# Two rotations of four PSUM banks in place of one of eight, in a context attention of small heads

## The chip, the cores and the metric

The kernel runs on one core of a Trainium2 chip. The metric is device time in microseconds (us) from one launch to its end, and the number compared is the median of several runs. The engines are TensorE (PE in the profile; its weight loads are shown apart as PEld), VectorE (DVE), ScalarE (ACT), GpSimd (POOL) and SyncE (SP), which issues the DMAs. Each engine takes its own instructions in order and waits on semaphores for the others. Matmuls write to PSUM, which here is used as eight banks of 128 partitions x 512 fp32 values; DVE and ACT read the results from there.

## What is computed

The program is a decoder of four layers for 4 sequences of 256 positions and width 128, all in fp32. Layers 0 and 2 have an attention over a context of 1601 positions of width 96, with 16 heads of 8. The change touches these two stages alone:

```python
def _L0_xattn_ref(x, context, context_mask, Wq, Wk, Wv, Wo):
    q = (x @ Wq).reshape(B, N, HEADS, hd).transpose(0, 2, 1, 3)
    k = (context @ Wk).reshape(B, M, HEADS, hd).transpose(0, 2, 1, 3)
    v = (context @ Wv).reshape(B, M, HEADS, hd).transpose(0, 2, 1, 3)
    scores = jnp.einsum('bhid,bhjd->bhij', q, k) * hd ** (-0.5)
    scores = jnp.where(context_mask[:, None, None, :], scores, max_neg)
    attn = jax.nn.softmax(scores, axis=-1)
    out = jnp.einsum('bhij,bhjd->bhid', attn, v)
    return out.transpose(0, 2, 1, 3).reshape(B, N, DIM) @ Wo
```

Layer 2's has biases on the queries, keys and values, and a two-layer ReLU network in place of `Wo`. After each comes a residual sum with a layer norm, and the next block of its layer.

## The kernel before, in words

The stages run one after the other (`setup`, `l0_attn`, `l0_xattn`, `block1`, `l2_xattn`, `l2_ffn`, `l3_attn`, `l3_xattn`). Each opens its own pools of buffers (`run`). Most stages, the two context stages `l0_xattn` and `l2_xattn` among them, have one PSUM pool of eight banks (L328), from which `misc()` hands out tiles named "one", each a whole bank, in turn. `acc()` is `misc()` cut to 256 columns. Pools keep a rotation for each name: a tile takes the buffer that was given out longest ago under that name, and its first matmul waits until the earlier tile there has been read by everything that reads it.

`context_heads` (L858) is called by both stages, with functions for the queries and for what follows the attention (`done`). Its work is 16 groups: a batch, one of two halves of the width, and one of two sets of 4 heads in that half. The four heads of a group lie in four strips of 32 rows (`SW`), so that a matmul of one head uses 32 rows of the PE array and matmuls of different heads can run beside each other. Each fp32 matmul is shown as two passes. A group is worked in three passes of seven steps:

- `maxima` (L907 to L931): scores of 128 queries against some 458 keys, one bank for each of the four heads; DVE reduces each bank to a maximum per query (L924; the last step of a group folds its parts at L930). The fourth of the seven steps (of `PARTS`) has two shorter pieces per head.
- `scores` (L933 to L948): the transposed scores of two chunks of 128 keys for all 256 queries, one bank per head, with the queries already shifted by the maximum; ACT takes the exponential from the bank into a tile "E" (L947).
- `sums` (L950 to L971): eight matmuls (16 passes) of the "E" tiles with the values, all four heads into one bank; ACT copies it out ("part", L968, or L965 for a group's first), and POOL adds it to the group's running sum (L969).

The main loop (L1002 to L1018) runs steps p. In each, the maxima belong to step p, the scores to step p - 9 and the sums to step p - 10, so up to three groups are under way. The order within a step is written out by hand: maxima of heads 0 and 1, scores of heads 2 and 3, scores of heads 0 and 1, maxima of heads 2 and 3, sums, and then at most a few other pieces: queries and keys of a later pair of groups (`keys`, copied by ACT at L885), values of a later batch, and `shift` (L985), which turns the maxima of a group by matmuls ("flips") and subtracts them from its queries on DVE (L561). `advance(later)` then moves the generators of finished groups on by one step each: `collected` (L845; flips, then DVE at L853 and L854), and for a finished batch `done`: projection or network, layer norm, and parts of the next blocks (in the first stage the queries of layer 1's attention, L1258, with a power on POOL at L1277). `manual_schedule` keeps this program order on PE, DVE and ACT. With maxima and scores of different heads next to each other, PE runs them at the same time in different strips.

So each stage begins with 9 steps of maxima without scores (the run-in) and ends with 10 without maxima (the run-out); between them 103 have maxima and scores, all but the first of these sums as well. In a step with everything the eight banks are given out in this order: two maxima, two scores, two scores, two maxima, the sums, and the other pieces. The ninth tile of a step, the sums, therefore takes the bank of that step's own first maximum, and a tenth that of the second.

Of the kernel before, what the change touches and what calls it, by code (L numbers as in the profile page):

```python
# [19 lines left out]
PSUM = bass.MemoryType.PSUM  # L20

B, T, D = 4, 256, 128
P = 128
# [280 lines left out]
class Net:  # L304
# [15 lines left out]
    def run(self, stage):  # L320
        with ExitStack() as ctx:
            def pool(name, bufs, **kw):
                return ctx.enter_context(
                    self.tc.tile_pool(name=f"{stage}{name}", bufs=bufs, **kw)
                )

            if stage in SINGLES:
                self.ps_one = pool("_one", 8, space=PSUM)  # L328
            else:
                self.ps_big = pool("_big", 3, space=PSUM)  # L330
                self.ps_one = pool("_one", 2, space=PSUM)
            self.stage = pool("", 2)
            getattr(self, stage)()
# [461 lines left out]
    def woven(self, run, lag):  # L795

        live = []
        for b in range(B):
            live.append((b * lag, run(b)))
        at = 0  # L800
        while live:
            for item in list(live):
                if item[0] <= at and next(item[1], self) is self:
                    live.remove(item)
            at += 1
# [52 lines left out]
    def context_heads(self, query, wk, wv, done):  # L858
# [48 lines left out]
        def maxima(i, p, jp):  # L907
            if p == 0 and jp == 0:
                ms[i] = self.tile("M", [P, NB, 4, 4], bufs=3)
            heads = [(j, self.misc()) for j in range(2 * jp, 2 * jp + 2)]  # L910
            at = 0
            for n, lo, hi in PARTS[p]:
                for j, ps in heads:
                    r = slice(SW * j, SW * j + KR)
                    self.mm(
                        ps[:, at : at + hi - lo], qs[i][r, n * P : (n + 1) * P],
                        ks[i // 2][r, lo:hi],
                    )
                at += hi - lo
            for j, ps in heads:  # L920
                at = 0
                for n, lo, hi in PARTS[p]:
                    part = p - 3 * n
                    nc.vector.reduce_max(  # L924
                        out=ms[i][:, n, j, part : part + 1], in_=ps[:, at : at + hi - lo], axis=AX.X
                    )
                    at += hi - lo
            if p == 6 and jp == 1:
                pad, at = self.next_mpad()
                nc.vector.reduce_max(out=at, in_=ms.pop(i), axis=AX.X)  # L930
                ms[i] = pad  # L931
# [69 lines left out]
        with self.tc.manual_schedule(engines=engines):  # L1001
            for p in range(-4, 7 * n_groups + 10):  # L1002
                (m, s, v) = (
                    divmod(p - lag, 7) if 0 <= p - lag < 7 * n_groups else None
                    for lag in (0, 9, 10)
                )
                if m:
                    maxima(*m, 0)
                if s:
                    scores(*s, 1)  # L1010
                    scores(*s, 0)
                if m:
                    maxima(*m, 1)
                if v:
                    sums(*v)
                for f, *args in other.pop(p, ()):
                    f(*args)
                self.advance(later)  # L1018
            while later:
                self.advance(later)  # L1020
# [42 lines left out]
    def l0_attn(self):  # L1063
        nc = self.nc

        def run(b):
# [55 lines left out]
            self.xT[b] = self.transposed(self.x[b], "xT", bufs=8, pool=self.act)  # L1122

        self.woven(run, 1)

    def project(self, b, tokens, w, bias=None):
# [1049 lines left out]
```

## Time and profile before

| | |
|---|---|
| time, median of 3 runs | 2635.44 us (2630.37, 2635.44, 2637.17) |
| the profiled execution's own time | 2632.08 us |
| its span | 2630.3 us |
| granted TensorE clock, mean | 0.976 |
| PE busy | 2461.2 us (94%) |
| DVE busy | 1742.6 us (66%) |
| ACT busy | 1565.4 us (60%) |
| POOL busy | 321.5 us (12%) |
| first context stage, 46 to 505 us | PE busy 423.43 of 459 us |
| second context stage, 768 to 1197 us | PE busy 407.15 of 429 us |

The profile is one execution. Its page gives the busy time of each engine, the chain of work that ended last as shares of the span, and groups of instructions: source line, engine, operation, the tiles written and read (`out<-in`) with their shapes, the count, the busy time and mean duration, and after the bar the idle time of that engine just before these instructions, with what ended it. The view of the waits adds such idle times up by engine, line and releaser: total in us, number, longest. The timeline lists instructions by start and duration; rows of the same kind close together are joined, with their count behind an x, and a bracket gives the idle time before and its releaser. Matmuls are pipelined, and their ends are modelled, so a matmul's shown end may lie a little after the next one's start.

How far apart the three parts of a stage lie is seen from stretches of the trace (length, then busy time and instructions of PE, PEld, DVE, ACT and POOL, granted clock, share of the DMA engines, GB/s). The first column is the stretch, in us from the span's start; run-in, middle and run-out of the first context stage, then of the second:

```profile
48.00:72.00 24.00, 23.10 (x243) 12.88 (x236) 20.70 (x43) 5.13 (x14) 0.00 (x0) 0.90 0.01 1
72.00:468.00 396.00, 372.16 (x5883) 236.43 (x5885) 284.61 (x654) 265.18 (x604) 87.86 (x94) 0.98 0.01 2
468.00:505.00 37.00, 26.17 (x413) 15.33 (x402) 3.85 (x12) 22.59 (x56) 19.12 (x13) 0.91 0.02 3
768.00:800.00 32.00, 27.77 (x456) 16.30 (x456) 27.96 (x66) 9.18 (x26) 4.82 (x7) 1.00 0.01 3
800.00:1172.00 372.00, 356.38 (x5732) 227.75 (x5724) 285.61 (x683) 254.62 (x591) 71.19 (x98) 1.00 0.02 5
1172.00:1197.00 25.00, 23.00 (x342) 12.34 (x336) 3.03 (x10) 20.91 (x51) 7.30 (x10) 1.00 0.01 2
```

PE is the busiest engine in every middle stretch; in the run-in of the first stage DVE has work for 20.70 of 24 us, in the run-outs ACT is nearly as busy as PE.

### The profile page before, as it was taken

Reading aid. Unit: us, or ns where it says so; the run is one execution under the profiler, and the core shown is the slowest. Engines: PE = TensorE matmul, PEld = TensorE weight load, DVE = VectorE, ACT = ScalarE, POOL = GpSimd, SP = SyncE. Lnnn points to the kernel's source line nnn. Section 1 sums busy time; section 2 is a strip of 40 time slices with the busy share of each in tenths; the row PEclk is TensorE's granted clock in tenths of the full one; section 3 lists DMA queues with packets and bytes.
Section 4 is the critical chain, followed back from the end, with each engine's and each line's share of the span. In section 5 each row is a group of like instructions: output and inputs, shape, how many; then the busy total and the mean of one; then the engine's idle time right before and its main releaser. Section 6 shows DMA issues by size and latency. Waiting matters only on the chain.

```text
span 2630.3 us, 70939 instructions
## 1 busy us (share of the span) xinstructions
PE 2461.2 (94%) x30079; PEld 1658.5 (63%) x30079; DVE 1742.6 (66%) x3802; ACT 1565.4 (60%) x3123; POOL 321.5 (12%) x393
## 2 busy tenths in 40 slices
PE   7998999798779999999999999999999999999997
PEld 4565656466546666657977777766566666666665
DVE  5776767365568777773556666657676776776775
ACT  2675766455436666675544555557675766666673
POOL 2113131410011111110010111010000000000000
PEclk9999999899989999999999999999999999999998
DMA  4000000000110000000021100000000000000000
GB/s 117 2 2 2 2 2 2 25 11 27 42 56 19 2 2 2 2 2 1 1 63 47 26 12 13 12 8 2 1 2 1 4 1 2 3 2 1 4 1 3
DMA packets 14716, 35.06 MB, mean 13 GB/s; under 512 B 4024, under 2 KB 7228, under 8 KB 13504
## 3 DMA queue, kind: packets, MB, share of 16 engines
q1 hardware_dynamic: 14400, 30.53, 4.2%
q8 instruction: 237, 3.88, 0.6%
q14 instruction: 79, 0.65, 0.1%
HBM read 23.67 MB, written 0.52 MB: 9 GB/s over the span
## 4 chain that ended last, share of the span: by engine, by line
PE 62%; DVE 7%; ACT 2%; issue 1%; POOL 0%; DMA 0%; POOLq 0%; DVEq 0%; ACTq 0%
PE one L404 46%; PE big L404 14%; DVE M L924 2%; PE one L411 2%; DVE St L2018 1%; DVE w L1984 0%; DVE rec L2066 0%; ACT E L746 0%; DVE ln_st L501 0%; DVE x L512 0%; ACT oT L492 0%; POOL ln_r L507 0%; DVE Q L1596 0%; DVE Ms L707 0%; DVE ln_mv L503 0%
## 5 line engine op out<-in xcount | busy, mean ns | idle before, releaser
L924 DVE TENSOR_REDUCE M<-one 128x1 f32<-128x458 f32 (+3 forms) x1024 | 512.5, 566 | 150.1 <-PE one L404 149.6
L947 ACT ACTIVATE E<-one 128x512 f32<-128x512 f32 (+1 forms) x896 | 435.5, 574 | 211.9 <-PE one L404 210.3
L404 PE MATMUL one<-K,Q 32*128 32x458 f32 (+3 forms) x2048 | 435.3, 527 | 0.6 <-DVE heads L854 0.6
L404 PE MATMUL one<-Q,K 32*128 32x256 f32 (+1 forms) x3328 | 397.6, 393 | 0.0
L1974 ACT COPY St<-big 128x1024 f32<-128x1024 f32 (+1 forms) x224 | 204.6, 959 | 154.6 <-PE big L404 154.4
L404 PEld LDWEIGHTS one<-Q,K 32*128 32x128 f32 (+1 forms) x3328 | 262.6, 182 | 34.5 <-issue 7.8
L404 PE MATMUL one<-E,V 128*32 128x256 f32 (+1 forms) x3328 | 229.5, 385 | 18.4 <-DVE M L924 17.2
L2018 DVE TENSOR_TENSOR St<-St,Mb 128x1024 f32<-128x1024 f32 (+1 forms) x224 | 245.3, 1142 | 1.8 <-ACT Mb L2012 1.8
L404 PEld LDWEIGHTS one<-K,Q 32*128 32x128 f32 x2048 | 177.5, 185 | 85.5 <-ACT part L968 28.9
L2025 ACT ACTIVATE St<-St 128x1024 f32<-128x1024 f32 (+1 forms) x224 | 215.1, 1014 | 25.4 <-DVE St L2018 25.3
L507 POOL TENSOR_TENSOR ln_r<-ln_ve,half 128x2 f32<-128x2 f32 x92 | 71.1, 773 | 1239.8 <-DVE ln_ve L505 1189.8
L746 ACT ACTIVATE E<-one 128x384 f32<-128x384 f32 (+1 forms) x352 | 154.2, 524 | 111.0 <-PE one L404 110.8
L969 POOL TENSOR_TENSOR acc_sb<-acc_sb,part 128x256 f32<-128x256 f32 x192 | 139.9, 728 | 623.5 <-ACT part L968 623.3
L404 PE MATMUL big<-Q,K 64*128 64x256 f32 (+1 forms) x1664 | 215.8, 394 | 0.0
L404 PE MATMUL one<-St,V 128*64 128x256 f32 (+1 forms) x1664 | 206.9, 384 | 0.4
L1984 DVE TENSOR_TENSOR w<-w,St 128x1024 f32<-128x1024 f32 (+1 forms) x160 | 178.6, 1116 | 34.3 <-ACT St L1974 27.2
L707 DVE TENSOR_REDUCE Ms<-one 128x3 f32<-128x384 f32 x256 | 130.2, 551 | 88.6 <-PE one L404 87.5
L404 PEld LDWEIGHTS big<-Q,K 64*128 64x128 f32 (+1 forms) x1664 | 148.6, 185 | 58.0 <-issue 40.8
L404 PE MATMUL one<-xT,w 128*128 128x256 f32 (+2 forms) x946 | 169.2, 394 | 15.2 <-DVE Q L1148 5.4
L404 PEld LDWEIGHTS one<-E,V 128*32 128x32 f32 (+1 forms) x3328 | 87.5, 109 | 144.2 <-DVE M L924 98.2
L404 PEld LDWEIGHTS one<-St,V 128*64 128x64 f32 (+1 forms) x1664 | 115.7, 137 | 62.3 <-issue 15.2
L404 PE MATMUL one<-QK 32*128 32x256 f32 (+1 forms) x1408 | 117.2, 385 | 19.8 <-ACT E L746 12.0
(338 smaller groups left out, 3919.7 us busy)
## 6 DMA issues: line engine op xcount, KB each, us to landing
QK<-qk SPq DMA_DIRECT2D x256, 16.0 KB
w<-in_p SPq DMA_DIRECT2D x12, 274.0 KB
rows<-in_ctx_rows SPq DMA_DIRECT2D x4, 630.5 KB
ctx<-in_ctx SPq DMA_DIRECT2D x4, 600.4 KB
w<-in_down SPq DMA_DIRECT2D x1, 2112.0 KB
w<-in_up SPq DMA_DIRECT2D x1, 1632.0 KB
w<-in_gp SPq DMA_DIRECT2D x1, 1632.0 KB
w<-in_p SPq DMA_DIRECT2D x4, 384.0 KB
```

The costliest lines, as they stand in the source:

```text
L404: self.nc.tensor.matmul(out[at], lhsT[:, at], rhs, start=start, stop=stop)
L411: self.nc.tensor.transpose(out, in_, self.ident)
L507: nc.gpsimd.tensor_tensor(rstd, ve, self.half[:, :NB], ALU.pow)
L707: nc.vector.reduce_max(out=m[:, j, :], in_=ps[:, : 3 * P].rearrange("p (s c) -> p s c", c=P), axis=AX.X,)
L746: nc.scalar.activation(es[t, j], ps[:, :w], AF.Exp, scale=scale)
L924: nc.vector.reduce_max(out=ms[i][:, n, j, part : part + 1], in_=ps[:, at : at + hi - lo], axis=AX.X)
L947: nc.scalar.activation(e[:kp, :w], ps[:kp, :w], AF.Exp, scale=scale)
L969: nc.gpsimd.tensor_add(accs[i], accs[i], part)
L1974: nc.scalar.copy(st[:kp, :, :nc_, :], ps[:kp, :, :nc_, :])
L1984: nc.vector.tensor_max(to, to, sts[u, k][:kp, :, :nc_, :])
L2018: nc.vector.tensor_sub(e, e, top[u][:kp].unsqueeze(2).broadcast_to([kp, 2, nc_, T]))
L2025: nc.scalar.activation(e, e, AF.Exp, scale=HD**-0.5)
```

## The change

The maxima's tiles get a name of their own, "top", and the pool of the two context stages holds four buffers for each name instead of eight for one. Eight banks are in use as before: four turn for the maxima, and four for the scores, the sums and every other piece of these stages (keys, queries, values, shifts, collected sums, and what follows them). Other stages keep their pools; `l3_xattn` has pools of another kind and does not call `context_heads`. The instructions of every engine are the same and in the same order; the buffers that they write, and so what they wait for, differ.

```diff
@@ -325,7 +325,7 @@
             if stage in SINGLES:
-                self.ps_one = pool("_one", 8, space=PSUM)
+                self.ps_one = pool("_one", 4 if stage[3:] == "xattn" else 8, space=PSUM)
             else:
                 self.ps_big = pool("_big", 3, space=PSUM)
                 self.ps_one = pool("_one", 2, space=PSUM)
@@ -907,7 +907,9 @@
         def maxima(i, p, jp):
             if p == 0 and jp == 0:
                 ms[i] = self.tile("M", [P, NB, 4, 4], bufs=3)
-            heads = [(j, self.misc()) for j in range(2 * jp, 2 * jp + 2)]
+            heads = [
+                (j, self.tile("top", [P, 512], pool=self.ps_one)) for j in range(2 * jp, 2 * jp + 2)
+            ]
             at = 0
             for n, lo, hi in PARTS[p]:
                 for j, ps in heads:
```

## The prediction

> **What bounds the kernel now.** I read the page first: engines, chain, groups.
>
> ```profile
> PE 2461.2 (94%) x30079; PEld 1658.5 (63%) x30079; DVE 1742.6 (66%) x3802; ACT 1565.4 (60%) x3123; POOL 321.5 (12%) x393
> ...
> PE 62%; DVE 7%; ACT 2%; issue 1%; POOL 0%; DMA 0%; POOLq 0%; DVEq 0%; ACTq 0%
> ...
> L924 DVE TENSOR_REDUCE M<-one 128x1 f32<-128x458 f32 (+3 forms) x1024 | 512.5, 566 | 150.1 <-PE one L404 149.6
> L947 ACT ACTIVATE E<-one 128x512 f32<-128x512 f32 (+1 forms) x896 | 435.5, 574 | 211.9 <-PE one L404 210.3
> ...
> L404 PE MATMUL one<-E,V 128*32 128x256 f32 (+1 forms) x3328 | 229.5, 385 | 18.4 <-DVE M L924 17.2
> ```
>
> PE is the bound, and both readers of the banks, the DVE maximum (L924) and the ACT exponential (L947), mostly wait for PE. PE's one visible wait on a bank is the last line: before the sums' matmuls (out "one", in "E,V") it stood idle 17.2 us in all, for DVE maxima. The waits of the first of the two context stages, from 60 to 480 us, say how often:
>
> ```profile
> DVE M L924 <- PE one L404: 78.1, 87, 2.0
> ...
> PE one L404 <- DVE M L924: 7.1, 8, 1.5
> ```
>
> Eight times in that stretch; 18 times (10.1 us) in the same stretch of the second stage. Next, the timeline of an ordinary step: start, duration, engine, and the count of instructions that a row joins.
>
> ```profile
> 292.45 0.54 ACT L885 COPY K<-one 128x458 f32<-128x458 f32 x1 [0.19 <-PE one L404]
> ...
> 293.38 2.26 DVE L924 TENSOR_REDUCE M<-one 128x1 f32<-128x458 f32 x4 [1.37 <-PE one L404]
> ...
> 293.56 2.06 ACT L947 ACTIVATE E<-one 128x512 f32<-128x512 f32 x4 [0.57 <-PE one L404]
> ...
> 293.83 0.38 PE L404 MATMUL one<-Q,K 32*128 32x256 f32 x2
> ...
> 294.16 1.07 PE L404 MATMUL one<-E,V 128*32 128x256 f32 x16
> ```
>
> Maxima and scores end at 293.83 + 0.38; the sums follow at once, at 294.16. One maximum takes 626 ns and one exponential 602 ns (groups split by shape), so the first maximum ends at 294.01 and the first exponential at 294.16. Before the change the sums' bank is that of the first maximum, 0.15 early; nothing is lost.
>
> **What the change does, part by part.** Each engine keeps its instructions and their order; no DMA, nothing of POOL's or SP's queue moves. Only banks move, so only what a matmul waits for. Maxima: four banks of their own, each last read a step earlier; that wait is over long before. Everything else turns round four banks. From the fourth piece to the fifth is one turn, so the sums take the bank of the *first scores of the same step*, and a further piece takes that of the second scores. In steps with one further piece the next step's second pair of scores takes the banks of the sums and of that piece; in steps without, that pair takes one score bank and the sums' bank.
>
> *1. Ordinary steps.* The sums start at 294.16, exactly when the first exponential ends; from now on they wait for it. What a release by ACT costs is to be seen where scores wait for an exponential today:
>
> ```profile
> 282.05 2.06 ACT L947 ACTIVATE E<-one 128x512 f32<-128x512 f32 x4 [0.52 <-PE one L404]
> ...
> 284.21 0.25 PEld L404 LDWEIGHTS one<-Q,K 32*128 32x128 f32 x3
> ```
>
> The fourth ends at 284.11, PE goes on at 284.21: 0.10. Behind the sums in PE's queue stand the further piece and the next step, with no gap, so the delay stays. I count 113 of the 204 steps (102 a stage) that have maxima, scores and sums with the sums 0.00 to 0.01 behind the exponential's end: 113 x 0.09 = +10.2. Bounds: 0.05, which a release by DVE costs (next fence: 1049.59 + 0.62 = 1050.21, PE at 1050.27), to 0.11: +5.7 to +12.4.
>
> *2. Three steps of the first stage* in which ACT is held up (L1217 waits for DVE, 6.9 us in three waits): there the first exponential ends 0.42 after the sums' start today: 3 x (0.42 + 0.10) = +1.6. Bounds 0 (a held-up ACT is made good at PE's next wait) to 1.6.
>
> *3. Steps in which DVE is late.* Other DVE work comes ahead of the maxima, and PE waits:
>
> ```profile
> 1048.83 2.06 ACT L947 ACTIVATE E<-one 128x512 f32<-128x512 f32 x4 [0.68 <-PE one L404]
> ...
> 1049.11 0.38 PE L404 MATMUL one<-Q,K 32*128 32x256 f32 x2
> ...
> 1049.59 2.25 DVE L924 TENSOR_REDUCE M<-one 128x1 f32<-128x458 f32 x4
> ...
> 1050.27 0.59 PEld L404 LDWEIGHTS one<-E,V 128*32 128x32 f32 x16 [1.18 <-DVE M L924]
> 1050.27 1.07 PE L404 MATMUL one<-E,V 128*32 128x256 f32 x16 [0.76 <-DVE M L924]
> ```
>
> With the change the sums go at 1049.43 + 0.10 = 1049.53 instead of 1050.27. What is late next: the next step's maxima, for which DVE is still busy. Single late steps are caught up: first stage 4 x 0.13 + 3 x 0.46 + 2 x 0.72 + 0.1 = 3.4, second stage 3.3. In the second stage three bursts (one from 1047 to 1059) would give 2.28 each, but DVE works through them without a pause; there the next maxima wait for DVE in place of the sums, and I keep 1.0 each. Sum -9.7. Bounds: 0 (DVE hands all of it back) to -17.2 (the page's whole row).
>
> *4. Run-in,* nine steps of maxima alone at each stage's start, DVE-bound (32 maxima without a pause, 50.67 to 66.16). PE ran up to eight banks ahead and hid the values' and keys' pieces; with four it stops earlier, and DVE idles while PE does those pieces. By the length of the pieces (0.6 to 1.0 each) +1.1 and +1.6 = +2.7. Bounds 0 (the lead is not needed) to +5.4.
>
> *5. Run-out,* ten steps without maxima at each stage's end, ACT-bound today:
>
> ```profile
> 1185.78 1.23 PE L404 MATMUL one<-E,V 128*32 128x256 f32 x16
> 1186.00 2.12 ACT L947 ACTIVATE E<-one 128x512 f32<-128x512 f32 x4
> ...
> 1186.93 1.16 PE L404 MATMUL one<-Q,K 32*128 32x256 f32 x16
> ```
>
> Period 2.24; the sums start before the same step's first exponential. With the change they wait for it, and the chain closes into a ring: exponential 0.60, release 0.10, sums 1.15 (1185.78 to 1186.93), first pair of scores 0.58, and about 0.2 to the next exponential: 2.63 to 2.65, or +0.41 a step. Of the twenty, five of the first stage lie under a POOL power of 10.56 us (L1277, 474.48 to 485.04) that holds PE until 486.59, and cost nothing while that cover stays. Fifteen x 0.41 = +6.2. Bounds 0 (ACT stays the bound) to 20 x 0.41 = +8.2.
>
> *6. Steps whose maxima come in two pieces,* some twelve: their scores wait for an exponential already (0.10, the fence above), so they take up what the sums lost before them: 12 x 0.09 = -1.0; 0 to -1.0. The second pair of scores after a key or collect copy: the copy ends at 292.99, the scores of that bank start at 293.29, so it still fits: 0, at most 0.2 x 60 such steps = +12.
>
> Sum: 10.2 + 1.6 - 9.7 + 2.7 + 6.2 - 1.0 = +10.0. The profiled execution took 2632.08 (span 2630.3), so 2642.1; it stands 3.4 under the median of 2635.44, against which I forecast 2645.4.
>
> [...]
>
> **Rivals.** *R1, faster.* PE is freed of DVE: all of part 3's 17.2 is kept, and ACT's release costs at most 0.05, as part 1's low end has it: 2632.1 + 5.7 - 17.2 = 2620.6 with parts 4 and 5 at 0, against the median 2624. For it: DVE is only 66% busy. Against it: the bursts. It decides once part 3 keeps more than parts 1, 2, 4 and 5 cost together. *R2, no difference:* gains and losses cancel within 7.9 us; part 3 at -17 with the rest as I have it gives +2.5, so 2638. *R3, much slower:* four banks are too few in ordinary steps too, since the second pair of scores has only about 0.3 to spare behind the further piece's copy, and less once the sums start later; 0.2 x 60 steps on top is +22, so 2657. Against it: the delay moves the scores as well. *R4, that it does nothing:* excluded; both context stages build the smaller pool, and the rotations differ as told.
>
> **How the numbers follow.** A measurement of this kernel tells about 0.3% (7.9 us) from no change. Forecast, slower by 8 to 20: 0.50; R3: 0.13; R2: 0.25; R1: 0.12. So faster 0.12, same 0.25, slower 0.63. The low ends of the parts together give 5.7 - 17.2 - 1.0 = -12.5, the high ends 12.4 + 1.6 + 5.4 + 8.2 + 12 = +39.6; neither is likely whole. The range cuts off most of R1 and the top of R3: 2628 to 2662.
>
> **What would show it.** Right: in ordinary steps the sums start 0.10 after the first exponential's end, and PE's and PEld's idle time before them stands to ACT L947, not to DVE L924; steps between 72 and 468 longer by about 0.09; run-out steps of 2.65; the row of 17.2 all but gone; busy times unchanged. Wrong: sums that start with the exponential's end or before it; run-out steps still of 2.24; scores idle for copies L885 or L968 (R3); the gap at 1050 gone without DVE waits behind it (R1).

## The result, and the profile after

The changed kernel takes 2650.61 us (median of 4 runs, 2645.75 to 2652.71), the kernel before beside it 2633.34 us (2630.37 to 2637.17): a ratio of 1.0062, 95% interval 1.0041 to 1.0083, or some 16 us slower (the two medians lie 17.3 apart). The forecast was 2645, with 2628 to 2662 as its range, and slower as the likeliest sign. So the time lies inside, but two of the parts that make it up were far off and partly made good for each other. The profiled execution took 2645.75 us, 13.7 more than the one before.

The page of the changed kernel, the lines that answer to those of before:

```profile
PE 2489.6 (94%) x30079; PEld 1681.4 (64%) x30079; DVE 1743.2 (66%) x3802; ACT 1566.7 (59%) x3123; POOL 321.2 (12%) x393
...
PE 65%; DVE 4%; ACT 1%; issue 1%; POOL 0%; DMA 0%; SPq 0%; POOLq 0%; DVEq 0%; ACTq 0%
...
L404 PE MATMUL one<-E,V 128*32 128x256 f32 (+1 forms) x3328 | 227.2, 387 | 6.3 <-ACT E L949 5.6
...
L404 PEld LDWEIGHTS top<-K,Q 32*128 32x128 f32 x2048 | 169.4, 185 | 91.0 <-DVE M L926 51.1
```

DVE's share of the chain fell from 7 to 4%. The 17.2 us that PE waited for DVE before the sums are gone, and ACT stands in that place now, with 5.6. PE's busy time grew by 28 us with the same instructions: they took longer, or ran side by side less. Weight loads of the maxima (now "top") wait for DVE, 51.1 us in all, where the same loads waited 17.1 before. Such a load goes ahead of its matmul, so this isn't idle time of PE: PE's matmuls themselves waited for a maxima bank three times, 3.8 us. Where each of these lies is seen in the timeline. An ordinary step of the changed kernel:

```profile
294.94 2.06 ACT L949 ACTIVATE E<-one 128x512 f32<-128x512 f32 x4 [0.57 <-PE one L404]
...
295.21 0.38 PE L404 MATMUL one<-Q,K 32*128 32x256 f32 x2
295.59 0.59 PEld L404 LDWEIGHTS one<-E,V 128*32 128x32 f32 x16 [0.40 <-ACT E L949]
```

The first exponential ends at 294.94 + 0.60 = 295.54, and the sums start at 295.59: they wait for ACT now, but the release costs 0.05 us, not 0.10. A step in which DVE is late, the counterpart of the one shown at 1050 us:

```profile
1060.88 2.06 ACT L949 ACTIVATE E<-one 128x512 f32<-128x512 f32 x4 [0.68 <-PE one L404]
...
1061.15 0.38 PE L404 MATMUL one<-Q,K 32*128 32x256 f32 x2
...
1061.53 1.07 PE L404 MATMUL one<-E,V 128*32 128x256 f32 x16
...
1061.64 2.25 DVE L926 TENSOR_REDUCE M<-top 128x1 f32<-128x458 f32 x4
```

The sums follow the scores at once, before DVE has begun; the gap of 0.76 is gone. Now the run-out of the second stage:

```profile
1199.10 2.06 ACT L949 ACTIVATE E<-one 128x512 f32<-128x512 f32 x4 [0.54 <-PE one L404]
...
1199.75 1.07 PE L404 MATMUL one<-E,V 128*32 128x256 f32 x16
...
1200.75 1.86 PE L404 MATMUL one<-Q,K 32*128 32x256 f32 x16
...
1201.98 2.06 ACT L949 ACTIVATE E<-one 128x512 f32<-128x512 f32 x4 [0.54 <-PE one L404]
```

The ring of the prediction is there, but a turn takes 2.88 us, not 2.65: exponential 0.60, release 0.05, sums 1.00, and 1.23 from the first scores to the next exponential. Before, the sixteen passes of a step's scores ran side by side in 1.16; now the second pair waits for its banks, and the passes are spread over 1.86. Last, DVE in the run-in of the first stage, first before the change and then after:

```profile
50.67 15.49 DVE L924 TENSOR_REDUCE M<-one 128x1 f32<-128x458 f32 x32 [4.68 <-PE one L404]
```

```profile
49.61 4.43 DVE L926 TENSOR_REDUCE M<-top 128x1 f32<-128x458 f32 x8 [4.25 <-PE top L404]
54.47 2.26 DVE L926 TENSOR_REDUCE M<-top 128x1 f32<-128x458 f32 x4 [0.44 <-PE top L404]
57.13 4.68 DVE L926 TENSOR_REDUCE M<-top 128x1 f32<-128x227 f32 x12 [0.40 <-PE top L404]
63.80 2.26 DVE L926 TENSOR_REDUCE M<-top 128x1 f32<-128x458 f32 x4 [1.99 <-PE top L404]
66.30 2.24 DVE L926 TENSOR_REDUCE M<-top 128x1 f32<-128x454 f32 x4 [0.24 <-PE top L404]
```

Thirty-two maxima in one piece before; after, DVE idles 0.44, 0.40, 1.99 and 0.24 between them, 3.1 us, because PE, with four banks of lead, does keys' and values' pieces while DVE has nothing left to read.

**The account by stretches.** DVE runs the same instructions in every kernel here, so the start of one DVE instruction can be compared between two traces. I cut the program at eight of them (in the trace before: 50.67, 78.72, 468.04, 503.32, 756.15, 803.37, 1170.21 and 1205.60 us) and give, for each stretch, its length less its length before. "Run-in 2" begins a little ahead of the second stage's first maxima. Each row is one profiled execution. What lies outside the columns (the first 50 us, and everything behind 1205 us, where no kernel here changes anything) moved by -1.1 to +5.3 and by -9.3 to -0.3 us from trace to trace, so a single trace's total says little. The columns say more, but the clock is in them too: run-in 1 is the same code in the changed kernel, e1, f2, g2, g3 and e5, and it reads +3.0 to +3.2 in three of these traces (mean granted clock of the stretch 0.95) and +6.7 to +6.9 in the other three (0.77 and 0.78). The last column is the measured ratio to the kernel before.

| kernel | run-in 1 | middle 1 | run-out 1 | block1 | run-in 2 | middle 2 | run-out 2 | ratio, 95% interval |
|---|---|---|---|---|---|---|---|---|
| length before, us | 28.05 | 389.31 | 35.29 | 252.83 | 47.22 | 366.84 | 35.39 | |
| the change | +3.0 | -0.7 | +5.9 | -2.5 | +7.9 | -2.5 | +7.1 | 1.0062 (1.0041 to 1.0083) |
| e1_sums_top | +6.8 | +0.2 | +3.5 | -0.3 | +4.7 | -0.5 | +3.7 | 1.0071 (1.0047 to 1.0095) |
| e2_run_in | +4.2 | -1.5 | +8.7 | -2.2 | +8.9 | -2.6 | +7.5 | 1.0080 (1.0063 to 1.0097) |
| e3_both_ends | +4.2 | -1.5 | +4.4 | +2.7 | +7.1 | -2.6 | +5.3 | 1.0088 (1.0071 to 1.0106) |
| e4_chosen | +0.2 | -2.5 | +4.4 | +0.1 | +7.4 | -5.2 | +5.3 | 1.0065 (1.0051 to 1.0079) |
| f1_ends_before | -0.4 | -0.8 | +0.2 | +0.1 | +4.9 | -2.3 | +1.7 | 1.0010 (0.9999 to 1.0021) |
| f2_middle_before | +6.9 | +0.1 | +4.5 | +7.5 | +5.7 | +0.3 | +6.6 | 1.0096 (1.0081 to 1.0111) |
| f3_all_turn | -0.7 | +0.4 | 0.0 | +0.1 | 0.0 | 0.0 | 0.0 | 0.9999 (0.9989 to 1.0010) |
| f4_best | -0.4 | -2.2 | +0.7 | +7.7 | +4.8 | -5.2 | +2.0 | 1.0006 (0.9991 to 1.0020) |
| g1_run_in_before | -0.4 | -0.6 | +6.0 | -2.6 | +5.1 | -2.6 | +7.2 | 1.0045 (1.0030 to 1.0061) |
| g2_run_out_before | +3.2 | +1.7 | +0.4 | +0.3 | +7.8 | -2.3 | +1.5 | 1.0050 (1.0031 to 1.0070) |
| g3_keep_busy | +6.7 | -0.8 | +2.3 | +0.3 | +5.6 | -2.6 | +7.0 | 1.0062 (1.0044 to 1.0080) |
| e5_second_exp | +3.0 | -0.9 | +5.9 | -2.6 | +8.0 | -2.6 | +6.4 | 1.0077 (1.0056 to 1.0098) |

In the changed kernel the two middles, some 200 steps, are 3.2 us *shorter*; the run-ins cost 10.9 and the run-outs 13.0 us.

### The profile page after: what moved, and what is told of

It reads as the page before. It is cut to its first block, busy times and chain, and to the rows that moved or that the text cites. A ratio compares the mean times of both kernels' runs of the same rounds, so it can differ in the third digit from the quotient of the medians.

```text
span 2644.0 us, 70965 instructions
## 1 busy us (share of the span) xinstructions
PE 2489.6 (94%) x30079; PEld 1681.4 (64%) x30079; DVE 1743.2 (66%) x3802; ACT 1566.7 (59%) x3123; POOL 321.2 (12%) x393
## 4 chain that ended last, share of the span: by engine, by line
PE 65%; DVE 4%; ACT 1%; issue 1%; POOL 0%; DMA 0%; SPq 0%; POOLq 0%; DVEq 0%; ACTq 0%
PE one L404 45%; PE big L404 14%; PE top L404 5%; PE one L411 2%; DVE St L2020 1%; DVE w L1986 0%; DVE rec L2068 0%; DVE M L926 0%; ACT E L746 0%; ACT oT L492 0%; DVE ln_st L501 0%; DMA QK<-qk 0%; POOL ln_r L507 0%; DVE Q L1598 0%; DVE Ms L707 0%
## 5 line engine op out<-in xcount | busy, mean ns | idle before, releaser
L926 DVE TENSOR_REDUCE M<-top 128x1 f32<-128x458 f32 (+3 forms) x1024 | 515.6, 567 | 155.2 <-PE top L404 152.2
L404 PE MATMUL top<-K,Q 32*128 32x458 f32 (+3 forms) x2048 | 442.5, 533 | 3.9 <-DVE M L926 3.8
L404 PE MATMUL one<-Q,K 32*128 32x256 f32 (+1 forms) x3328 | 423.6, 395 | 1.5 <-DVE heads L854 1.0
L404 PEld LDWEIGHTS one<-Q,K 32*128 32x128 f32 (+1 forms) x3328 | 297.5, 183 | 37.6 <-issue 8.4
L404 PEld LDWEIGHTS top<-K,Q 32*128 32x128 f32 x2048 | 169.4, 185 | 91.0 <-DVE M L926 51.1
```

The lines of the kernel that those rows point to most:

```text
L404: self.nc.tensor.matmul(out[at], lhsT[:, at], rhs, start=start, stop=stop)
L926: nc.vector.reduce_max(out=ms[i][:, n, j, part : part + 1], in_=ps[:, at : at + hi - lo], axis=AX.X)
```

## The experiments

**The sums in the maxima's banks.**

```diff
-            acc = self.acc()
+            tag = "top"
+            acc = self.tile(tag, [P, 512], pool=self.ps_one)[:, :T]
```

> The sums' tile goes to the maxima's four banks; scores and all other pieces keep their four. Against the kernel before, the changed kernel's trace shows three sums: run-ins +8.3 us (3.0 and 5.3), middles -2.6 (-1.1 and -1.5), run-outs +12.3 (6.3 and 6.0). Theory (which bank a tile waits for decides): in every step the sums wait for a DVE maximum again, so run-out steps go back from 2.88 to 2.2 us, the 17 us of idle PE in DVE-late steps come back, and only the run-ins' cost stays: 2633 + 8 = 2641 us (2637 to 2646). Rival (four banks are too few for the scores and the other pieces, whatever the sums take): run-out steps stay near 2.9 us, and the time at 2648 us or more.

Measured: 2645.35 us against 2628.81, ratio 1.0071, about 19 us: the rival's side. In the middles the theory holds (+0.2 and -0.5: the gain in the late steps and the cost in the others are both gone). The run-outs do not come back. The sums wait for no exponential there, yet:

```profile
1204.33 2.06 ACT L949 ACTIVATE E<-one 128x512 f32<-128x512 f32 x4 [1.15 <-PE one L404]
...
1205.88 1.69 PE L404 MATMUL one<-Q,K 32*128 32x256 f32 x16
...
1207.11 2.06 ACT L949 ACTIVATE E<-one 128x512 f32<-128x512 f32 x4 [0.45 <-PE one L404]
```

That step takes 2.78 us, and the next 2.62. With four banks the scores of a step can only begin as the last step's exponentials release theirs one by one, and the passes come apart (1.69 instead of 1.16). So the run-out's loss has two causes: the sums' wait, and four banks for the scores, which cost without it. In the second stage +3.7 us of the changed kernel's +7.1 stay. Some of the difference is the clock's: the mean granted clock of that stretch is 1.00 here, as before the change, and 0.92 in the changed kernel, and f1 (below), with the old order there and 0.95, shows +1.7. Of the 5.4 us between the changed kernel and f1 the scores' four banks are, by these traces, the larger part.

**Mending the ends, first try.** The run-in's maxima take the other four banks in odd steps (e2); with that, the sums of the run-out go to the maxima's banks (e3); with that, the sums of the middle take a maxima's bank in all steps but 31 (e4).

```diff
+            step = 7 * i + p
+            tag = "one" if step < 9 and step % 2 else "top"
             heads = [
-                (j, self.tile("top", [P, 512], pool=self.ps_one)) for j in range(2 * jp, 2 * jp + 2)
+                (j, self.tile(tag, [P, 512], pool=self.ps_one)) for j in range(2 * jp, 2 * jp + 2)
             ]
...
-            acc = self.acc()
+            tag = "top" if 7 * i + k + 10 >= 112 else "one"
+            acc = self.tile(tag, [P, 512], pool=self.ps_one)[:, :T]
```

The last three lines are e3's; in e4 the condition is that the step is not one of the 31 in which DVE was late before.

> In the run-in (steps 0 to 8 of each stage) the maxima of odd steps take the other four banks, so PE has eight banks to run ahead again; all else as in the changed kernel. Theory (the run-ins' +8.3 us are PE's lost lead over DVE): the run-ins are as long as before the change, 2650.6 - 8 = 2642 us (2638 to 2646); run-out steps stay at 2.88 us. Rival (the run-ins are longer for another reason, the granted clock or the wait for the stage before): they stay as they are, 2648 to 2652 us.

> The run-in as in the run-in kernel, and from step 112 on the sums take the maxima's banks, which stand free then; the middle is as in the changed kernel. Theory: both ends are as long as before the change, and the middle's -2.6 us stay: 2633 - 3 = 2630 us (2626 to 2634). Rival (the middle costs 0.09 us a step, as predicted, and its shorter look in the trace is a gain of another place): 2640 us or more.

> As the kernel of both ends, and in the middle the sums take a bank of the maxima in all steps but the 31 in which DVE was late before the change; in those they take a score bank. Theory: the ordinary steps' wait for ACT (0.045 us in 113 steps, 5 us) goes, the gain in the late steps (some 7.6 us) stays: 2633 - 7.6 = 2626 us (2622 to 2630), under both kernels. Rival (five tiles a step in the maxima's four banks make the maxima wait for DVE): no better than the kernel of both ends, 2630 to 2640 us.

Measured: 1.0080, 1.0088 and 1.0065, that is 21, 23 and 17 us over the kernel before: three misses. These edits did not bring the old order back. In the run-in the keys' and values' pieces still go through the four banks "one", which now hold the odd steps' maxima, so a piece waits until DVE has read those. In the kernel of chosen banks PE stood still for 4 us in the second run-in:

```profile
787.56 0.99 PE L411 MATMUL one<-ctx,w 97*32 97x227 f32 x8 [4.02 <-DVE M L935]
```

Run-in 1 is the same code in all three, and there the clock is a rival to this account: it reads +4.2 in e2 and e3, at a mean granted clock of 0.84, and +0.2 in e4, at 1.00. What the three do show is the middle: with the chosen banks it is 2.5 and 5.2 us shorter than before the change.

**The old order exactly, stretch by stretch.** If every tile takes the two names in turn, each name's four banks come round every eight tiles: the rotation of eight again. A condition in the main loop says where this holds: in both ends (f1), in steps 9 to 111 alone (f2), everywhere (f3), and in both ends with the chosen banks of the middle (f4).

```diff
-    def misc(self):
-        return self.tile("one", [P, 512], pool=self.ps_one)
+    def misc(self, tag="one"):
+        if self.turn:
+            self.turned += 1
+            tag = ("one", "top")[self.turned % 2]
+        return self.tile(tag, [P, 512], pool=self.ps_one)
...
-            heads = [
-                (j, self.tile("top", [P, 512], pool=self.ps_one)) for j in range(2 * jp, 2 * jp + 2)
-            ]
+            heads = [(j, self.misc("top")) for j in range(2 * jp, 2 * jp + 2)]
...
             for p in range(-4, 7 * n_groups + 10):
+                self.turn = p < 9 or p >= 7 * n_groups
```

> All tiles take the two names in turn in the run-in (up to step 8) and from step 112 on, which is one rotation of eight again, as before the change; steps 9 to 111 are as in the changed kernel. Theory (the loss is in the two ends: PE stalls there, and where it stalls the granted clock falls, which the runs before this one showed from 768 to 790 and from 480 to 500): the ends' +20 us go and the middle's -2.6 stay: within 5 us of the kernel before, at or under it. Rival (the ends are only where slow stretches of the clock happen to fall, and the change costs its time in the middle): 10 us or more over the kernel before.

> The other half: one rotation of eight in steps 9 to 111, two rotations of four in the run-in and from step 112 on. Theory of the ends: as slow as the changed kernel or a little slower, 16 to 22 us over the kernel before. Rival (the middle costs the time): within 5 us of the kernel before.

> The two names in turn everywhere in the two stages: the bank order of the kernel before, with the changed kernel's two names. Every theory expects the time of the kernel before, within 0.3%, and full clock from 768 to 790 if that stretch's clock follows from the bank order. If the slow clock there turns up in this kernel too, it falls by chance, and the traces' differences at the ends are partly that.

> The ends in one rotation of eight; in the middle four banks for the maxima, and the sums take a bank of the maxima except in the 31 steps in which DVE was late before, where they take a score bank. In the kernel of chosen banks the middles were 3.0 and 5.2 us shorter than before the change. Theory of the ends: 2628.8 - 8 = 2621 us on that chip, 3 to 10 us under the kernel before. Rival (the ends are long for another reason): 5 us or more over it.

Measured: f1 1.0010 (+2.6 us, its interval reaches just below 1), f2 1.0096 (+25), f3 0.9999, f4 1.0006 (+1.6). That settles the place. With the old order in the ends alone the loss is gone; with the old order in the middle alone it stays; with the old order everywhere the time is that of the kernel before. f2 is 9 us over the changed kernel, of which its longer middles explain 3.5; what else is longer in its trace lies in run-in 1, where it has the changed kernel's code, and in block1, which is the same code in all kernels. f4's middles are 7.4 us shorter, yet its time is not shorter: its trace has +7.7 us in block1 and +4.8 in run-in 2. The granted clock is what differs there: its mean over block1 is 0.88 in f4 and in f2, 0.91 before the change and 0.93 after it. That is more than one trace's chance, since f4's twelve runs have a mean granted clock of 0.968 to 0.975 and the 29 of the kernel before beside them 0.973 to 0.979; why f4 comes out lower no run settles. The stretches of the trace from 768 us on, before the change, after it, in f1 and in f3 (columns as in the table of stretches above: the clock is third from the end):

```profile
768.00:778.00 10.00, 7.54 (x121) 3.94 (x122) 6.22 (x18) 2.25 (x5) 4.82 (x7) 1.00 0.01 2
778.00:792.00 14.00, 13.03 (x247) 8.06 (x246) 13.77 (x34) 4.49 (x17) 0.00 (x0) 1.00 0.01 3
```

```profile
768.00:778.00 10.00, 8.08 (x67) 3.06 (x70) 2.39 (x7) 1.14 (x3) 4.67 (x6) 0.50 0.01 2
778.00:792.00 14.00, 11.29 (x120) 5.36 (x116) 8.43 (x21) 1.81 (x4) 0.69 (x1) 0.75 0.01 1
```

```profile
768.00:778.00 10.00, 8.08 (x82) 3.16 (x77) 2.03 (x6) 1.00 (x3) 4.67 (x6) 0.53 0.01 2
778.00:792.00 14.00, 12.14 (x156) 7.29 (x144) 10.11 (x24) 3.40 (x11) 0.70 (x1) 0.76 0.01 1
```

```profile
768.00:778.00 10.00, 8.08 (x113) 3.68 (x115) 3.30 (x10) 2.08 (x5) 4.67 (x6) 0.85 0.01 2
778.00:792.00 14.00, 11.19 (x204) 6.71 (x200) 13.03 (x36) 3.51 (x12) 0.69 (x1) 1.00 0.01 2
```

f1 has the old order in this run-in, and half clock all the same. So the +4.9 us that f1 shows there do not come from the run-in's banks; only the other 3 of the changed kernel's +7.9 do. g1 (next), also with the old order there, reads +5.1, and e5 and g2, with the changed kernel's, +8.0 and +7.8, all five at a mean granted clock of 0.84 or 0.85 over the stretch (before the change 0.96); with the changed kernel's order at 0.90, e1, f2 and g3 read +4.7 to +5.7.

**Each end by itself.** The same condition for the run-in alone (g1: `p < 9`) and from step 112 on alone (g2).

> One rotation of eight up to step 8 of each stage, the rest as in the changed kernel. The kernel with the old order at both ends stands 2.6 us over the kernel before, the changed kernel 16.4. Theory (the run-ins cost some 10 us: PE's lost lead, and the slow clock that follows its pauses): 6 to 9 us over the kernel before; the first stage's run-in as long as before the change, in the second the half clock may still fall into the run-in. Rival (the run-outs carry nearly all): 14 us or more over it.

> One rotation of eight from step 112 of each stage on, the rest as in the changed kernel. Theory (the run-outs cost some 10 us, by the ring of sums and exponentials): steps of 2.2 us there again, 8 to 12 us over the kernel before. Rival (the run-ins carry nearly all): 14 us or more over it.

Measured: 1.0045 (+12 us) and 1.0050 (+13 us), each near the midway between theory and rival; g1 lies over its theory's range, g2 a little over. By the stretches each mends what it was to mend: run-in 1 goes from +3.0 to -0.4, run-out 1 from +5.9 to +0.4, run-out 2 from +7.1 to +1.5. Each end carries a share, and neither carries nearly all; the two gains against the changed kernel (4 and 3 us) do not add up to that of both together (14), but their intervals, some 4 us either way, do not say how much of that is real.

**Keeping PE busy through a pause.**

```diff
+        self.name = stage
...
+            if i == 14 and self.name == "l0_xattn":
+                for _ in range(7):
+                    junk = self.tile("top", [P, 512], pool=self.ps_one)
+                    self.mm(junk, self.ident[: CD + 2], self.ctx_all[:, :512])
             self.collected(sb, at[:, :, kt, :, r, :], 8, 8 * r)
```

> The changed kernel, with seven unneeded products of 98 x 128 by 98 x 512 into banks of the maxima put on PE just before the flips that wait for the long POOL power in the first stage's run-out; nothing reads them. Theory (PE's pause of 5 us and more there is followed by half clock, to about 498 us in the changed kernel, and that is part of the run-out's +6 us): PE is busy to about 486 us, the granted clock stays 1.00 to 500 us, and the steps after the pause take 2.65 to 2.9 us instead of up to 4.4: 3 to 4 us less than the changed kernel, in spite of the added work. Rival (the waits alone make the run-out long): no less than the changed kernel.

Measured, the place: PE of the changed kernel around the POOL power, and then of this kernel.

```profile
488.58 1.08 PE L404 MATMUL one<-c,acc_sb 128*32 128x128 f32 x16 [5.70 <-POOL acc_sb L971]
489.59 2.79 PE L404 MATMUL one<-Q,K 32*128 32x256 f32 x16
492.41 1.94 PE L404 MATMUL one<-E,V 128*32 128x256 f32 x16
494.28 2.69 PE L404 MATMUL one<-Q,K 32*128 32x256 f32 x16
...
507.48 0.62 PE L404 MATMUL one<-E,V 65*32 65x256 f32 x8
```

```profile
492.23 6.19 PE L405 MATMUL top<-ctx,c 98*32 98x512 f32 x56
498.24 0.62 PE L405 MATMUL one<-c,acc_sb 128*32 128x128 f32 x16
498.80 1.85 PE L405 MATMUL one<-Q,K 32*128 32x256 f32 x16
500.67 1.07 PE L405 MATMUL one<-E,V 128*32 128x256 f32 x16
501.67 1.86 PE L405 MATMUL one<-Q,K 32*128 32x256 f32 x16
...
513.35 0.62 PE L405 MATMUL one<-E,V 65*32 65x256 f32 x8
```

From the flips to the last sums it is 18.90 us in the one (507.48 - 488.58) and 15.11 in the other, 3.8 less, by 6.19 us of matmuls that nobody needs. The sixteen passes of flips take 1.08 and 0.62. The stretches of 2 us show a granted clock of 0.50 from 486 to 498 in the changed kernel, and of 1.00 throughout here; those of the flips, in the one and in the other:

```profile
488.00:490.00 2.00, 1.42 (x19) 1.00 (x22) 0.24 (x2) 0.00 (x0) 0.53 (x1) 0.50 0.00 0
```

```profile
498.00:500.00 2.00, 2.00 (x34) 1.65 (x31) 1.00 (x4) 0.00 (x0) 0.07 (x1) 1.00 0.00 0
```

So the pause does slow what follows. The whole time, 2645.51 us and 1.0062, shows no gain over the changed kernel; 3.8 us is not more than the interval holds, and this trace has +6.7 in run-in 1.

**The wait for the sums, made longer.**

```diff
+            if jp == 1:
+                heads = [(2, heads[1][1]), (3, heads[0][1])]
```

> The changed kernel with the banks of the second-listed heads' scores (heads 2 and 3) given out in the other order, so that the sums take the bank whose exponential is the second to end, 0.49 us later; no instruction moves. Theory (the sums start 0.05 us after the exponential that reads their bank ends): 0.49 us in each of some 130 steps, less what is made up in steps that wait already, 50 to 65 us over the changed kernel. Rival (which bank does not matter, only how many there are): no difference.

Measured: 1.0077, and a step as in the changed kernel: an ordinary one has its first exponential at 299.63, which takes 0.60, and its sums at 300.28, still 0.05 behind the first exponential and not behind the second. So the edit did not move the sums to another bank, and it decides nothing. That fits banks going out in the order in which tiles are first used, not in which they are asked for: exchanging two tiles before either is used then exchanges their names alone. It serves as a second measurement of the changed kernel, and its row in the table repeats the first within 0.7 us in all columns.

## Why the prediction was right, and where it was not

The sign, the place of the sums' wait and the ring in the run-out were right, and so was the reason for the middle: one bank's release decides there, not the number of banks. At the ends the number decides as well (e1). That the total came near is in part luck. Parts 1, 2, 3 and 6 make +1.1 us for the middles, which came out 3.2 *shorter*: steps longer by 0.09, one of the signs of being right, did not come, and PE's busy time, to be unchanged, grew by 28 us. "Slower" came true by the ends alone, which cost twice their forecast. The sizes:

*Part 1, ordinary steps, and part 2.* Predicted +10.2 and +1.6. The release by ACT that I took, 0.10, came from a step of two-piece maxima; before the sums it is 0.05, which I had as the lower bound. f4 and the changed kernel differ in the middle in which bank the sums take, so by this wait above all, at 1.5 and 2.7 us: +4.2 for both parts in place of 11.8. That is the term oversized.

*Part 3, late steps.* Predicted -9.7 (3.4 and 6.3); f4, whose sums take the bank that is free first, has -2.2 and -5.2, together -7.4. What the bursts would hand back was sized about right.

*Part 4, run-in.* Predicted +1.1 and +1.6. Measured against f1, which has the old order: 3.4 in the first stage and 3 in the second. I counted the pieces' lengths at full clock; the piece that left DVE idle for 1.99 us was followed by eight passes of maxima that took 1.91 us (the granted clock was 0.50 from 61.4 to 64.8 us), 1.05 elsewhere. And 3.4 is the lower of two readings: the same code gives +6.7 to +6.9 in the traces of e1, f2 and g3, where the clock of that stretch is 0.77 or 0.78. Five traces with the old order there have no such reading; whether the four banks' pauses bring it on or chance does is open.

*Part 5, run-out.* Predicted +0.41 a step, +6.2 (4.1 of it in the second stage). Measured: +5.8 and +5.4 against f1; a turn of the ring takes 2.88 instead of 2.24, +0.64, in three of the second stage's turns; four others take 2.33 to 2.77. The failed step is "first pair of scores, 0.58": I halved the 1.16 that four heads take, but the four run side by side, and two alone take as long (1.13 from the first pass's start to the last's end at 1200.75): 1.23 with what lies up to the exponential, where I had 0.78. And e1 shows that without the sums' wait the scores' four banks alone make a step of up to 2.78. The first stage's 5.8 has another cause besides: of its steps outside the POOL power, the turns after the pause take 4.69, 3.45, 2.87 and 2.33 in the changed kernel, and 2.87, 2.87, 2.87 and 2.33 in g3, where the clock stays 1.00; before the change they took 2.18 to 2.22. At full clock that is +2.2, close to the 2.1 forecast for that stage; another 2.4 is half clock.

*Part 6.* The second pair of scores after a copy cost nothing that the middles show; R3 is out. The -1.0 of the steps with two pieces no run takes apart from the rest.

*What no part had:* the granted clock. Its half rate fell into the second run-in in the changed kernel (+5 us), lasted longer in the first run-out (in part 5), and fell out of block1 (-2.5 us).

*R1* fell at the ends, not in the middle, where PE does gain from being rid of DVE (-3.2). The ends cost some 17.5 us against f1 (3.4 + 3 + 5.8 + 5.4), twice the 8.9 of parts 4 and 5. With -3.2 for the middles that makes some 14, which is what f1's ratio and the changed kernel's leave between them. The clock's +5 and -2.5 make it some 17, where 16 were measured, but that agreement is not to be leaned on: these are single traces, the changed kernel's 4.9 us under the median of its runs and f1's 5.8 above.

That all eight banks are in use as before holds for the middle. At the ends it does not: in the run-in the scores' banks, and in the run-out the maxima's, serve hardly anything, and there each chain has four banks where it had eight. f1 shows what that costs in this kernel: 16 us less 2.6.

## What to carry to other kernels

A fixed split of buffers is paid where one side has nothing to do: look at the run-in and run-out of a software pipeline apart from its middle, however few steps they have, since 38 of the 244 steps here lost some 17 us while the rest gained 3. When a wait is moved from one engine to another, take the release's price from a step of the same kind (0.05 us here, where I had taken 0.10), and do not halve the time of matmuls that ran side by side (1.16 us for four heads, 1.13 for two). Here stretches of half clock shifted together with the pauses of PE, in code that nobody touched too (block1 read -2.5 us at a mean granted clock of 0.93 and +7.7 at 0.88), so a few us in an untouched stretch of one trace are no evidence for or against an edit.

## What was not expected of the hardware

In stretches of 2 us the granted clock of PE reads 1.00 or 0.50 at these places, with values between only where it changes, and half clock begins there behind pauses of PE of 1.86 to 2.89 us, though not behind one of 1.85. The lines are of the changed kernel, behind block1's last steps, and the last of f1, which has the old order in this run-in:

```profile
767.32 0.49 PE L411 MATMUL one<-c,x 128*128 128x128 f32 x2 [2.88 <-DVE x L512]
...
771.85 1.08 PE L404 MATMUL one<-xT,w 128*32 128x256 f32 x8 [0.72 <-DVE heads L854]
...
783.79 3.42 PE L404 MATMUL top<-K,Q 32*128 32x458 f32 x8 [2.71 <-DVE M L926]
```

```profile
783.09 0.59 PE L409 MATMUL top<-ctx,w 97*32 97x227 f32 x8 [1.86 <-DVE M L929]
```

After the pause of 2.88 us the eight passes at 771.85 take 1.08; before the change they took 0.64, behind a pause of 2.89 us at 762.65. By the 2 us stretches half clock held from about 762.6 to 766.0 before, 3.4 us, and from 768.0 to 778.2 after, 10.2 us, behind the same pause. The pause of 2.71 at 783.79, which the change made, was followed by some 6.8 us of half clock, to 791.9. The length of the pause doesn't decide that here: the one in its place before the change, 1.85, was followed by none, and f1's, 1.86, by the same 6.8 us, to 791.1. What the traces before and after the change share is the lengths. Their record of the granted clock knows 1.00 and 0.50 alone, and its stretches of 0.50, but for the one at the program's end, last 3.41, 6.83, 10.24, 13.65 or 20.48 us, that is one, two, three, four or six times the shortest (17 stretches before, 16 after); in each of the two traces their starts lie multiples of 3.4133 us apart, to within 0.005 us. Why it was 10.2 us in the one trace and 3.4 in the other no run settles.
